# Expert order by group, and twelve picked steps instead of six, in a graph layer with a mixture of experts

## The chip, the cores and the metric

The kernel runs on one core of one Trainium2 chip. The metric is the device time of one execution in microseconds (us). The engines are named as the profile names them: PE (TensorE matmuls; its weight loads are PEld), DVE (VectorE), ACT (ScalarE), POOL (GpSimd) and SP (SyncE). ACT and SP also issue plain DMAs, each on a queue of its own, and POOL issues the indirect ones (gathers and scatters of rows).

## The reference, cut to what matters

A layer over 3,125 nodes with 256 features and 100,000 edges, sorted by destination. After a layer norm, an edge network gives every node the maximum over its incoming edges, a linear mixer runs over all nodes, and both are added to the input. Then comes a mixture of eight experts, of which every node takes its two best:

```python
xn = _layernorm(x, axis=-1)
x = x + gnn(xn, src, dst) + mix(xn)          # gnn: segment_max over the edges of relu(...)
xt = _layernorm(x, axis=-1)
probs = softmax(xt @ Wr + br); top_p, top_idx = top_k(probs, 2)
h = gelu(einsum('end,edh->enh', xe, W1) + b1)      # E = 8 experts, 256 -> 1024
y = einsum('enh,ehd->end', h, W2) + b2             # 1024 -> 256
out = x + (weights[:, :, None] * sel).sum(axis=1)  # the two chosen experts of each node
```

All data are float32. The weights of one expert (W1 and W2) are 2 MB.

## The kernel before

**Edges.** The edges lie in reverse order of their destination, so that nodes with high numbers are finished first. They are cut into four groups of columns, `STEPS = (263, 209, 157, 98)`; the nodes are handled in the groups `GROUPS = ((11, 25), (4, 11), (1, 4), (0, 1))` of tiles of 128 nodes. For each step POOL gathers 128 rows of a table `b_d` into a window `g` (line 111), and DVE folds it into a running maximum (`fold`, line 386). A window holds up to eight steps; SP stores it to `s_d` in DRAM once it is folded (`folding`, line 1457). There are five window buffers (`WN`). After the last step of a group, `last_rows` gathers from `s_d` the row at which each node ends (tile `r`), `carry` takes maxima across the 128 lanes (lines 393 to 410), and `token_tile` adds everything up, normalizes, and computes the routing.

**The last group of edges** belongs to node tile 0 alone. Its last six steps (`KEPT = 6`) are not stored. A row that ends in one of them is picked by a matmul instead: `last_ends` makes one 128x128 matrix of ones and zeros for each such step (line 1364, in `end_ones(j)`), sums them with matmuls of one column (line 1369) to learn which nodes end there, and `pick_ends` multiplies the matrix with the folded rows, accumulating in one bank (line 1381). ACT reads the sum as `kept` (line 1386), and DVE takes the maximum of it and the gathered `r` (line 459).

**Experts.** The class `Stream` runs the experts of node groups 0, 1 and 2. A lot is 256 rows of one expert in groups 0 and 1 (two lots an expert in group 0) and 128 rows in group 2. So there are 24 uses of an expert, numbered q = 0 to 23, with the experts in order 0 to 7 in each group. One unit of `Units.run` has eight steps: in each, PE makes a piece of the hidden layer (`hp`, line 644), ACT applies gelu (line 646), and PE adds a piece of the second product of the unit before (`yp`, line 668). In step 4, PE brings in the rows of the next unit (`trf`); in group 2 these are picked from chip by matmuls (line 739) with matrices that DVE makes (line 730). The bias of the second product is line 812, and ACT copies the result out (line 813).

There are three weight buffers: `w` and the two halves of `big`. Use q has buffer q mod 3. At step 7 of use q, `next_w(q + 2)` asks for the weights of use q + 2, in four parts of 512 KB (two of W1, two of W2); the ACT queue issues one part at step 7 and the others at steps 0, 2 and 5 of the next unit, right behind the gelu of that step. Every one of the 24 uses loads its 2 MB.

Node tile 0 comes last and runs all eight experts densely (`dense_tile`), in the order `DENSE = (5, 6, 7, 0, 1, 2, 3, 4)`: 5, 6 and 7 still lie in the three buffers, and five experts are loaded for it. Meanwhile `combine` gathers for the other nodes the two expert results (`g<-ys_d,from_i`), DVE adds them (line 1402), and SP writes `out`.

**Order.** PE, DVE, ACT and SP follow an order written out when the program is built: a clock of the builder ticks with each gather, tasks are due at given times, and `room()` spaces the units by an estimate of PE's time. Each engine then runs its list strictly in order. POOL has its own order of gathers (`behind`). Every plain DMA has one of eight completion counters in turn, and a DMA is issued when the last one on its counter has landed.

Of the kernel before, what the change touches and what calls it, by code (L numbers as in the profile page):

```python
# [14 lines left out]
OP = mybir.AluOpType  # L15
# [4 lines left out]
P = 128  # L20
# [4 lines left out]
D = 256  # L25
# [8 lines left out]

DENSE = (5, 6, 7, 0, 1, 2, 3, 4)
# [20 lines left out]
KEPT = 6  # L56
# [15 lines left out]
def gps_layer(ctx: ExitStack, tc: tile.TileContext, x, src, dst, thetaT, phiT, gbias, wq, wkvT,  # L72
# [608 lines left out]
    class Stream:  # L681


        def __init__(self, wts, act, ps):
            self.wts, self.act, self.ps = wts, act, ps
            self.lots, self.through, self.open = [], set(), True
            self.held = {}
            self.parts = []

        def add(self, g):  # L690
            self.lots += [(g, e, h) for e in range(E) for h in range(CAPS[g] // LOT[g])]
# [6 lines left out]
        def two(self, what, v):  # L698

            g, e, h = self.lots[2 * v]  # L700
            rows = what[g][e * CAPS[g]:e * CAPS[g] + 2 * LOT[g]]
            return rows.rearrange("(k p s) d -> p k s d", p=self.half(2 * v), k=2 * LOT[g] // CAPS[g])
# [29 lines left out]
        def turn(self, u):  # L732
            if ("hot", u) in self.held and ("tr", u) not in self.held:
                tr = self.held["tr", u] = self.ps.tile([P, 2, ROWS], F32, name="trf", bufs=1)
                i0, i1 = GROUPS[G - 2]
                hot = self.held["hot", u]
                for c in range(2):
                    for i in range(i0, i1):
                        nc.tensor.matmul(tr[:, c, 0:CAPS[G - 2]], xn2(i)[:, c * P:(c + 1) * P], hot[:, i - i0, :],
                                         start=(i == i0), stop=(i == i1 - 1))  # L740
                on_pe(1.5)
                if u + 1 == len(self.lots):
                    dense_half(0, 0, xn_lo[:, 1:1 + FC, :].rearrange("p i d -> p (i d)"), nc.scalar)
            elif ("xs", u // 2) in self.held and ("tr", u) not in self.held:
                tr = self.held["tr", u] = self.ps.tile([P, 2, ROWS], F32, name="trf", bufs=1)
                n = self.half(u)
                for c in range(2):
                    for r in range(2):
                        nc.tensor.transpose(tr[:, c, r * n:(r + 1) * n],  # L749
                                            self.held["xs", u // 2][0:n, u % 2 * 2 + r, c * P:(c + 1) * P],  # L750
                                            ident[0:n, 0:n])
                on_pe(1.2)
# [9 lines left out]

        def next_w(self, q, parts=None):
            if q < (G - 1) * E:
                self.held["w", q] = load_w(self.wts[q % 3], q % E, nc.scalar, parts)
# [5 lines left out]
        def more_w(self):  # L771
            while "firsts" not in clock:
                yield 1
            for k in range(1, 3):
                self.next_w(k)
                yield 25

        def go(self):
            units = Units(self.ps, self.act)
            u, q = 0, -1  # L780
            self.next_w(0)
            start(self.more_w())
            yield 25
            while True:
# [24 lines left out]
                def done(r, yp, u=u, ys=ys):  # L809
# [3 lines left out]
                    nc.scalar.copy(ys[0:n, u % 2 * PARTS[g] + r, :], yp[0:n, :])  # L813
# [10 lines left out]
                if h == 0:  # L824
                    q += 1
                    if q:
                        between[7] = lambda: (self.next_w(q + 2, self.parts), self.part())
# [3 lines left out]
                w1t, w2t = self.held["w", q]  # L831
# [3 lines left out]
            for k in range(3):  # L835
                dense_w[DENSE[k]] = self.held["w", q - 2 + k]
# [123 lines left out]
    def loads():  # L960
# [18 lines left out]
        move(nc.scalar, kept[:, STEPS[G - 1] - KEPT:STEPS[G - 1], :], zero.to_broadcast([P, KEPT, D]))  # L979
# [349 lines left out]
    dense_w = {}  # L1329

# [5 lines left out]
    def next_dense(k):  # L1336

        if k < 3:
            e = DENSE[k + 5]
            dense_w[e] = load_w(at_hand["w"][k], e, nc.scalar)  # L1340
# [3 lines left out]
    def end_ones(j):  # L1344
        of = xn_lo[:, SPLIT - 2:SPLIT, :] if j < 4 else xn_hi[:, 12:14, :]
        return of.rearrange("p i (c k) -> p (i c) k", k=P)[:, j % 4, :]

    def last_ends():
# [14 lines left out]
        for j in range(KEPT):  # L1363
            nc.vector.tensor_scalar(end_ones(j), row, float(1 + P * COL[g] + STEPS[g] - KEPT + j), None, op0=OP.is_equal)
            yield 1
        yield 2
        here_p = mm.tile([P, 1], F32, name="mm")
        for j in range(KEPT):
            nc.tensor.matmul(here_p, end_ones(j), ones[:, 0:1], start=(j == 0), stop=(j == KEPT - 1))
# [7 lines left out]
    def pick_ends(j, rows):  # L1377
# [3 lines left out]
        nc.tensor.matmul(ends["p"][:, 0:D], end_ones(j), rows, start=(j == 0), stop=(j == KEPT - 1))  # L1381
        on_pe(0.5)
        if j == KEPT - 1:
# [51 lines left out]
    def starts(g):  # L1435

        most = STEPS[g] - KEPT
        n = -(-most // W)
        at = [most * k // n for k in range(n + 1)] + [most + 4, STEPS[g]]
        if g == G - 1:  # L1440
            at.remove(most + 4)
        return [(a, b - a) for a, b in zip(at, at[1:])]

    def folding():

        for g in range(G):
            last = None
            rows = s_d[1 + P * COL[g]:1 + P * COL[g + 1], :].rearrange("(p t) d -> p t d", t=STEPS[g])
            for w, (t0, n) in enumerate(starts(g)):
                for j in range(n):  # L1450
# [3 lines left out]
                    if g == G - 1 and t0 + j >= STEPS[g] - KEPT:  # L1454
                        start(pick_ends(t0 + j - STEPS[g] + KEPT, last), clock["now"] + 0.5)
                if g < G - 1 or t0 + n < STEPS[g]:
# [204 lines left out]
```

## Time and profile before

| what | value |
|---|---|
| time, median of 3 runs | 1211.97 us (1210.92 to 1213.29) |
| time of the profiled execution | 1210.82 us |
| its span (first to last instruction) | 1209.0 us |
| mean granted TensorE clock | 0.86 |
| busy share of PE, PEld, DVE, ACT, POOL | 80%, 55%, 63%, 28%, 71% |
| DMA over the span | 305.46 MB, 253 GB/s |
| 512 KB parts of expert weights: issues on `big`, on `w` | 56, 28 |
| last gather of `b_d` rows starts | 1102.90 us |
| first matmul of an expert, group 0 / group 1 / group 2 | 594 / 881 / 1036 us |
| first expert matmul of the dense tile | 1136.55 us |
| last result of the dense tile on DVE | 1202.71 us |

How to read it: in the timeline a row is one run of equal instructions with its start and its length in us, and in brackets the idle time before it and what ended it. The chain of waits goes back from the last instruction to whatever released it. Windows give the busy time of each engine in a stretch, then the granted clock, the busy share of the DMA engines and the GB/s that they moved. PE counts a float32 matmul as two passes, so that a step of the hidden layer (two matmuls) shows as x4.

### The profile page before, as it was taken

To read this page: it belongs to the slowest core of one execution; us is meant where nothing else is said; L and a number is where in the kernel's file an instruction comes from. 1 tells how busy PE (TensorE), PEld (TensorE's weight loads), DVE (VectorE), ACT (ScalarE), POOL (GpSimd) and SP (SyncE) were. 2 spreads that over 40 slices of the span, in tenths; PEclk is the share of its full clock that TensorE was granted. 3 is DMA by queue.
4 is the path that set the end of the run, shared out by engine and by line. 5 is a ranking of instruction groups with operands and counts; after the bars stand their busy time and mean duration, and the time that the engine had idled before them with its cause. 6 is when DMAs were issued, how large, how long until landed. Compare 5 with 4: busy or idle time off the path is not lost.

```text
span 1209.0 us, 13723 instructions
## 1 busy us (share of the span) xinstructions
PE 967.2 (80%) x4062; PEld 670.0 (55%) x4062; DVE 758.9 (63%) x2255; ACT 333.4 (28%) x796; POOL 854.7 (71%) x879
## 2 busy tenths in 40 slices
PE   6428888787389445586599999999889999889796
PEld 5314443343144123332388888877678886778696
DVE  7698898899977999934333331786433336543443
ACT  4301232222011012311233333333133334333241
POOL 6677777777777477777777776774777767774734
PEclk9758998889579655568699999999989998889898
DMA  8756776655765755664668897774889996999593
GB/s 276 248 164 211 280 264 204 220 184 195 235 223 200 266 176 172 237 240 168 197 222 319 305 308 253 258 273 171 286 294 351 375 349 228 331 395 382 174 353 118
DMA packets 96366, 305.46 MB, mean 253 GB/s; under 512 B 19798, under 2 KB 39503, under 8 KB 85658
## 3 DMA queue, kind: packets, MB, share of 16 engines
q0 software_dynamic: 42400, 115.28, 30.4%
q1 hardware_dynamic: 25564, 107.09, 22.7%
q10 hardware_dynamic: 28318, 82.13, 19.2%
q8 instruction: 34, 0.56, 0.2%
q14 instruction: 50, 0.41, 0.1%
HBM read 183.66 MB, written 120.75 MB: 252 GB/s over the span
## 4 chain that ended last, share of the span: by engine, by line
PE 56%; DVE 20%; DMA 9%; issue 9%; POOL 2%; ACT 2%; ACTq 0%; DVEq 0%; SPq 0%; POOLq 0%
PE hp L644 17%; PE yp L668 16%; DVE g L386 5%; DVE ring L1108 4%; PE mm L423 3%; DMA g<-b_d,srcI 3%; DMA big<-in_w 3%; PE yp L812 2%; POOL g L111 2%; PE k L1140 2%; PE bp L261 2%; PE k L1080 2%; PE v L1140 2%; PE banks L1104 2%; PE mm L421 1%
## 5 line engine op out<-in xcount | busy, mean ns | idle before, releaser
L111 POOL DMA_INDIRECT g<-b_d,srcI x727 | 712.2, 980 | 227.2 <-issue 192.7
L386 DVE SCALAR_TENSOR_TENSOR g<-g,cut 128x256 f32<-128x256 f32 x723 | 349.9, 484 | 238.3 <-DMA g<-b_d,srcI 227.2
L646 ACT ACTIVATE ring<-hp,sm 128x256 f32<-128x256 f32 (+1 forms) x320 | 137.8, 432 | 297.9 <-PE hp L644 294.5
L644 PE MATMUL hp<-xe,big 128*128 128x256 f32 (+1 forms) x800 | 180.7, 351 | 10.1 <-DMA big<-in_w 5.1
L668 PE MATMUL yp<-big,ring 128*128 128x256 f32 x640 | 169.3, 382 | 0.0
L644 PEld LDWEIGHTS hp<-xe,big 128*128 128x128 f32 x800 | 140.8, 199 | 34.5 <-issue 13.6
L668 PEld LDWEIGHTS yp<-big,ring 128*128 128x128 f32 x640 | 115.3, 190 | 18.0 <-issue 5.6
L1108 DVE CUSTOM_DVE_ANT_0 ring<-big,banks 128x1024 bf16<-128x1024 f32 (+1 forms) x102 | 101.6, 996 | 24.5 <-PE banks L1104 24.3
L668 PE MATMUL yp<-w,ring 128*128 128x256 f32 x352 | 100.7, 406 | 0.0
L644 PE MATMUL hp<-xe,w 128*128 128x256 f32 (+1 forms) x416 | 96.1, 359 | 2.5 <-DMA w<-in_w 1.4
L644 PEld LDWEIGHTS hp<-xe,w 128*128 128x128 f32 x416 | 73.0, 197 | 14.9 <-issue 3.9
L668 PEld LDWEIGHTS yp<-w,ring 128*128 128x128 f32 x352 | 67.7, 203 | 11.5 <-issue 3.6
L111 POOL DMA_INDIRECT g<-ys_d,from_i x48 | 46.4, 966 | 31.0 <-DMA out<-g 16.8
L1104 PE MATMUL banks<-ring,row_of 16*128 16x512 bf16 (+1 forms) x90 | 30.7, 415 | 44.1 <-DVE big L1108 44.1
L1104 PEld LDWEIGHTS <-row_of 16*128 16x128 bf16 x112 | 7.7, 97 | 80.9 <-DVE big L1108 54.3
L111 POOL DMA_INDIRECT r<-s_d,end_i x25 | 24.5, 979 | 39.5 <-DMA s_d<-g 22.9
L760 ACT ACTIVATE xe<-trf,sm 128x256 f32<-128x256 f32 (+1 forms) x64 | 30.8, 535 | 40.6 <-PE trf L749 32.4
L749 PE MATMUL trf<-ident,xn_hi 128*128 128x128 f32 x96 | 15.4, 286 | 31.2 <-DMA xn_hi<-xs_d 31.2
L812 PE MATMUL yp<-b_sb,ident 8*128 8x256 f32 x112 | 39.3, 431 | 0.0
L1104 PE MATMUL trf<-ring,row_of 16*128 16x512 bf16 (+1 forms) x22 | 11.6, 525 | 34.2 <-DVE big L1108 34.2
L1140 PE MATMUL v<-wkv,xn_hi 128*128 128x512 f32 x56 | 33.7, 733 | 2.7 <-ACT vn L1145 2.4
L1152 ACT ACTIVATE rsk<-var,eps 128x16 f32<-128x16 f32 x25 | 7.7, 308 | 100.2 <-DVE var L1149 100.2
(316 smaller groups left out, 1363.2 us busy)
## 6 DMA issues: line engine op xcount, KB each, us to landing
s_d<-g SPq DMA_DIRECT2D x73, 1024.0 KB, 4.7
big<-in_w ACTq DMA_DIRECT2D x56, 512.0 KB, 7.6
s_d<-g SPq DMA_DIRECT2D x17, 896.0 KB, 5.0
w<-in_w ACTq DMA_DIRECT2D x28, 512.0 KB, 9.3
g<-b_d,srcI POOLq DMA_INDIRECT x727, 3.8
big<-in_w ACTq DMA_DIRECT2D x4, 2048.0 KB
xn_hi<-xs_d ACTq DMA_DIRECT2D x12, 512.0 KB, 5.2
xs_d<-zero ACTq DMA_DIRECT2D x8, 512.0 KB, 4.9
```

The costliest lines, as they stand in the source:

```text
L111: got = nc.gpsimd.indirect_dma_start(out=to, out_offset=None, in_=table, in_offset=row_index(index))
L261: nc.tensor.matmul(bp, xnT(i, c), wb[:, c, :], start=(c == 0), stop=(c == 1))
L386: nc.vector.scalar_tensor_tensor(g[:, j, :], last, cut[:, t:t + 1], g[:, j, :], op0=OP.add, op1=OP.max)
L423: nc.tensor.matmul(am, xnT(i, c), am_w[:, c, :], start=False, stop=False)
L644: nc.tensor.matmul(hp[:, 0:n], w1t[:, c, f, :], xe[:, c, 0:n], start=(c == 0), stop=(c == 1))
L646: nc.scalar.activation(hT[f][:, 0:n], hp[:, 0:n], AF.Gelu, bias=sm[:, 4 + f, e:e + 1])
L668: nc.tensor.matmul(yp[r][0:part, :], hT[q][:, r * part:(r + 1) * part], w2t[:, q, :], start=(q == 0), stop=(q == FC - 1 and self.whole))
L760: nc.scalar.activation(xe[:, c, 0:n], self.held["tr", u][:, c, 0:n], AF.Identity, bias=sm[:, 2 + c, e:e + 1], scale=sm[:, c, e:e + 1])
L812: nc.tensor.matmul(yp[0:n, :], ident[0:E, e:e + 1].to_broadcast([E, n]), b2_sb, start=False, stop=True)
L1104: nc.tensor.matmul(mask_p[:, at:to], row_of[:, k:k + 1].to_broadcast([FIRST, P]), no_edge[:, i0 * P + at:i0 * P + to], start=True, stop=True)
L1108: nc.vector.tensor_tensor_reduce(unread[:, 0:n], bT[:, h, i0 * P:i0 * P + n], mask_p[:, 0:n], 1.0, NEG, op0=OP.add, op1=OP.max, accum_out= ...
L1140: nc.tensor.matmul(to, xnT(i, c), wkv[:, c, k * INNER:(k + 1) * INNER], start=(c == 0), stop=(c == 1))
```

## The change

Two things are changed at once.

The order of the experts differs by group (`ORDERS`). Group 0 ends with experts 5, 6 and 7 on chip, and group 1 now begins with 6, 7, 5; group 1 ends with 1, 2, 3 on chip, and group 2 begins with 2, 3, 1. `plan()` works out at build time which of the three buffers holds which expert at each use and which use issues a load. Loads are still asked for two uses ahead, at step 7. The uses 8, 9, 10 and 16, 17, 18 load nothing. Group 2 ends with 5, 6, 7 as before, and the dense tile takes them from the buffers in which they now lie (`dense_slot`).

The last group of edges keeps its last twelve steps on chip instead of six (`KEPT_LAST`): the last two windows, of six steps each, are not stored, and twelve matrices are made, summed and multiplied. The matrices of the further steps lie in `xn_hi`. The rows of `s_d` that are never written are filled with zeros early on, for twelve steps instead of six.

```diff
+ORDERS = ((0, 1, 2, 3, 4, 5, 6, 7), (6, 7, 5, 4, 0, 1, 2, 3), (2, 3, 1, 0, 4, 5, 6, 7))
-KEPT = 6
+KEPT, KEPT_LAST = 6, 12
...
         def add(self, g):
-            self.lots += [(g, e, h) for e in range(E) for h in range(CAPS[g] // LOT[g])]
+            self.lots += [(g, e, h) for e in ORDERS[g] for h in range(CAPS[g] // LOT[g])]
...
+        def plan(self):
+            uses = [e for order in ORDERS for e in order]
+            self.uses, self.slot, self.loads = uses, {}, {}
+            at = [None] * 3
+            for q in range(-3, len(uses)):
+                self.loads[q] = []
+                ahead = [k for k in range(max(q, 0), len(uses)) if uses[k] not in at]
+                if ahead:
+                    wanted = set(uses[max(q, 0):ahead[0]])
+                    free = [k for k in range(3) if at[k] not in wanted]
+                    if free:
+                        at[free[0]] = uses[ahead[0]]
+                        self.loads[q].append((uses[ahead[0]], free[0]))
+                self.slot[q] = {e: k for k, e in enumerate(at) if e is not None}
         def next_w(self, q, parts=None):
-            if q < (G - 1) * E:
-                self.held["w", q] = load_w(self.wts[q % 3], q % E, nc.scalar, parts)
+            for e, k in self.loads.get(q, ()):
+                self.held["w", k] = load_w(self.wts[k], e, nc.scalar, parts)
...
-                        between[7] = lambda: (self.next_w(q + 2, self.parts), self.part())
+                        between[7] = lambda q=q: (self.next_w(q, self.parts), self.part())
...
             for k in range(3):
-                dense_w[DENSE[k]] = self.held["w", q - 2 + k]
+                dense_w[DENSE[k]] = self.held["w", self.slot[q][DENSE[k]]]
+                dense_slot.append(self.slot[q][DENSE[k]])
...
-        move(nc.scalar, kept[:, STEPS[G - 1] - KEPT:STEPS[G - 1], :], zero.to_broadcast([P, KEPT, D]))
+        move(nc.scalar, kept[:, STEPS[G - 1] - KEPT_LAST:STEPS[G - 1], :], zero.to_broadcast([P, KEPT_LAST, D]))
...
     def end_ones(j):
+        if j >= 8:
+            return xn_hi[:, 0:4, :].rearrange("p i d -> p (i d)")[:, 384 + (j - 8) * P:384 + (j - 7) * P]
...
-        for j in range(KEPT):
-            nc.vector.tensor_scalar(end_ones(j), row, float(1 + P * COL[g] + STEPS[g] - KEPT + j), None, op0=OP.is_equal)
+        for j in range(KEPT_LAST):
+            nc.vector.tensor_scalar(end_ones(j), row, float(1 + P * COL[g] + STEPS[g] - KEPT_LAST + j), None, op0=OP.is_equal)
...
-        nc.tensor.matmul(ends["p"][:, 0:D], end_ones(j), rows, start=(j == 0), stop=(j == KEPT - 1))
+        nc.tensor.matmul(ends["p"][:, 0:D], end_ones(j), rows, start=(j == 0), stop=(j == KEPT_LAST - 1))
...
     def starts(g):
-        most = STEPS[g] - KEPT
+        kept = KEPT_LAST if g == G - 1 else KEPT
+        most = STEPS[g] - kept
         n = -(-most // W)
-        at = [most * k // n for k in range(n + 1)] + [most + 4, STEPS[g]]
-        if g == G - 1:
-            at.remove(most + 4)
+        at = [most * k // n for k in range(n + 1)] + [most + (6 if g == G - 1 else 4), STEPS[g]]
...
-                if g < G - 1 or t0 + n < STEPS[g]:
+                if g < G - 1 or t0 < STEPS[g] - KEPT_LAST:
                     move(nc.sync, rows[:, t0:t0 + n, :], wins[g, w][:, 0:n, :])
```

## The prediction

> **What bounds the kernel now.** I read the table of slices first, then windows by stage, then the chain of waits from group 2 on, then PE's timeline there. In groups 0 and 1 PE is full (79.84 of the 80 us from 600 to 680, 128.01 of the 130 us from 885 to 1015) and no step waits for a weight part; the gap at 861 to 881 us is a wait for `xn_hi<-xs_d`, with no weights in flight. Loads saved before 1030 us can't shorten that. Group 2 is different. The chain (start us, length us, what):
>
> ```profile
> 1054.46 12.07 DMA big<-in_w
> 1066.66 0.78 PE hp L644 x2
> 1067.47 11.80 DMA big<-in_w
> 1079.40 0.47 PE hp L644 x2
> 1079.91 10.16 DMA w<-in_w
> 1090.20 0.47 PE hp L644 x2
> 1090.70 9.68 DMA big<-in_w
> 1100.52 0.46 PE hp L644 x2
> ...
> 1117.37 3.65 PE yp L668 x16
> 1121.02 0.62 PE yp L812 x2
> 1121.65 2.80 PE am L1381 x12
> 1124.47 0.48 ACT kept L1386
> 1125.00 1.57 PE am L465 x6
> ```
>
> Four times PE waits for a weight part and then starts a use with a lone half step. From one start of such a part's flight to the next are 13.0, 12.4, 10.8 and 10.3 us (1054.46, 1067.47, 1079.91, 1090.70, 1100.98). A use that doesn't wait takes 9.2: in PE's timeline (start, length) use 18 begins at the first row below, and the last row of its step 7 is followed by 1062.83.
>
> ```profile
> 1049.84 0.95 PE L1369 MATMUL mm<-ones,xn_lo 128*128 128x1 f32 x8
> 1050.65 0.58 PE L1369 MATMUL mm<-ones,xn_hi 128*128 128x1 f32 x4
> ...
> 1053.65 0.71 PE L644 MATMUL hp<-xe,w 128*128 128x128 f32 x4
> ...
> 1062.21 0.69 PE L812 MATMUL yp<-b_sb,ident 8*128 8x256 f32 x2
> ```
>
> So the four periods hold 46.5 - 4 x 9.2 = 9.8 us of waits (3.8, 3.2, 1.6, 1.1). The DMA engines are full there. Of the 25.83 MB moved from 1037 to 1105 us, the ACT queue, which carries the weights, has this (packets, MB, share):
>
> ```profile
> q10 hardware_dynamic: 4083, 13.44, 52.8%
> ```
>
> That is 198 GB/s for weights; a use in 9.2 us wants 2.097 MB, 228 GB/s. The other queues move 12.3 MB, 181 GB/s.
>
> After the last use the chain runs through picks, `kept`, the last carry and the routing, to the dense tile at 1136.55. The dense phase moves with its start, but for one stall (DVE and POOL rows; what stands in brackets is the idle time and what ended it):
>
> ```profile
> 1168.12 0.95 POOL L111 DMA_INDIRECT g<-ys_d,from_i  x1 [16.48 <-DMA out<-g]
> ```
> ```profile
> 1181.49 0.48 DVE L1402 SCALAR_TENSOR_TENSOR g<-g,share 128x256 f32<-128x256 f32 x1 [2.11 <-DMA g<-ys_d,from_i]
> 1181.89 0.60 DVE L863 TENSOR_SCALAR xe<-xT,sm 128x128 f32<-128x128 f32 x2
> ```
>
> PE's next dense step stands behind that L863: it comes 3.74 us late, and three steps at half clock follow (1.71 against 0.88), 2.5 us more.
>
> **The loads.** The built order of the changed kernel has 24 parts fewer on the ACT queue, so the saving is real: six loads of four parts. Those of uses 8, 9, 10 lie where nothing waits: 0. Those of 16, 17, 18 lie ahead of the waits, and seven of their parts (3.67 MB) move in 1037 to 1050. The loads that PE waits for, 19 to 22, all stay, asked for with the same lead; what goes is the backlog ahead of them. Is that enough? From about 1051, when the first is asked for, to use 23's second W1 part are 4.5 loads, 9.44 MB: at 198 GB/s 47.7 us, so 1098.7, and about 2 to land, 1101. Unwaited, use 18 starts at 1052.4 (1.25 before 1053.65, as L1369 leaves use 17) and use 23 follows after five uses of 9.2, the 2.5 of L1369 below, and 2.5 for one stretch of half clock, as at 1064.8 to 1071.6 (an estimate: three steps at 1.71 instead of 0.88): 1103.4. So the waits close with 2.4 us to spare. Single parts can still be late: of the remainder, between 0 and 9.8, I take 1.0. At 228 GB/s nothing would wait; at 175 GB/s the stretch would be 54 us, and use 23 some 4 late.
>
> Can the engines give more than 380 in all? Windows (length, busy us and rows of PE, PEld, DVE, ACT, POOL, then clock, DMA share, GB/s):
>
> ```profile
> 1055.00:1080.00 25.00, 20.80 (x123) 18.03 (x122) 12.08 (x31) 7.54 (x22) 18.39 (x20) 0.86 1.03 399
> 1105.00:1110.00 5.00, 5.00 (x36) 4.23 (x35) 2.49 (x8) 2.07 (x6) 0.00 (x0) 1.00 1.04 415
> ```
>
> With 399 the weights would have 218 (399 less 181), with 415 they would have 234. The row nearest in place is the first; I keep 198, as measured over the whole stretch, for the sum, and the others for the fast side.
>
> A rule speaks against the change here. The Trainium skill, "DMA: Bandwidth & Descriptors", section "Where 436 GB/s comes from", puts the HBM limit of a core at about 358 GB/s for transfers from HBM. By that figure weights would keep 177 GB/s, the stretch would take 53 us and use 23 would be some 3 us late instead of in time, for a sum near -3. The windows above show 399 and 415, so in this trace the measurement decides.
>
> **Added on PE.** The sum of the matrices (L1369) has 24 passes for 12 and moves from use 17 to use 18: the 12 take 1049.84 to 1051.09, so +1.25, on the path as PE runs its list in order. Where PE would wait for weights anyway it costs 0, that is the other end. It waits on the DVE's matrices, six more at about 0.22 us (L1364), placed between folds of 0.48 us that follow gathers 1.25 us apart: taken as 0, 1.3 if they were in the way. Behind it on PE stand the steps of use 18 and gelu.
>
> The picks (L1381) have 24 passes for 12; the 12 took 2.80 in the chain (with the last fold long done: it ends at 1108.96). Of the twelve picks, two now fall in use 23, four among the last `yp` and six at the end; nothing hides them, since PE is full from 1101 on: +2.7. Below that is 0, if use 23 waits for its weights. The last L812 (0.62) goes from before the picks to behind six of them and the carry's transpose (L393): the same sum.
>
> On ACT `kept` now stands behind the copy of the last result (0.37) and the issue of `ys_d` (0.38), which stood ahead of it before too, but during the picks: +0.8; between 0 (if the copy falls under the carry's matmul) and 1.1.
>
> **Moved elsewhere.** SP has one store fewer, so `r` can be gathered sooner. Before, POOL waits:
>
> ```profile
> 1117.62 0.94 POOL L111 DMA_INDIRECT r<-s_d,end_i  x1 [13.77 <-DMA s_d<-g]
> ```
>
> The `ys_d` gathers behind it come some 8 to 10 us sooner. But the carry takes `r` only at 1125, released by `kept`, and DVE's adds (L1402) stand behind the dense start in its list: 0. What covers `r`: the carry would come near 1120, a gather takes 3.8 us from issue to landing (the page's median of the edge gathers), and its issue should come near 1108 to 1110. If the store let it start only after 1116, each further microsecond would count. POOL's own list is unchanged. In the dense stall fewer gathers are in flight while `out<-g` lands: four of 131 KB, at the 345 GB/s of 1150 to 1180 1.5 us. The stall can stay (0) or go with its half clock (-6.3); I take -1.0, as the 14 us landing of that store is set by 2 MB of `g<-in_w` ahead of it on SP's queue, which stay. The zero fill writes 0.75 MB more at 54 to 108 us, where POOL's gathers set the pace: 0; at 200 GB/s it would be under 3.8 us if it stood alone.
>
> **The sum**, against the profiled execution of 1210.82 (span 1209.0 and 1.82 around it): -9.8 + 1.0 + 1.25 + 2.7 + 0.8 - 1.0 = -5.05, so 1205.8. The median of the runs is 1.15 above the profiled one: 1206.9, called 1207.0.
>
> **Rivals.** (B) The weights still pace uses 21 to 23. The gathers and stores come at POOL's rate whatever PE does, and a faster PE asks for weights sooner; each use then falls short by 10.6 - 9.2 = 1.4 us, and the first W1 parts may land 4 us late. With waits of w = 4 to 6 left the sum is -2 to 0: 1210 to 1212, no measurable change. For it: the same four loads, the same lead, 52.8% share. Against: 7.0 of the 9.8 us lie in the first two periods, right behind the removed loads.
>
> (C) Slower. All the waits stay, because a part's flight (9.7 to 12 us) comes from sharing the engines with gathers and stores, not from the backlog. The flights shrink only from 12.07 to 9.68 along the group, though the removed parts are long gone by the last. Then w = 9.8 and the added 4.75 on PE and ACT is paid in full: 1216.7. It decides from w = 5.05 on (without the -1.0), and is measurable from w = 7.5, 1214.4. Against: a part that lands late delays only a use that has no slack, and the first one now starts with more.
>
> (D) The dense stall goes too, since the `ys_d` gathers have 8 us more: -5 - 5, about 1202. Against: its cause is a store behind loads on SP's queue, both of which follow the dense start.
>
> **How the numbers follow.** Forecast 0.45, B 0.24, C 0.17, D 0.14. About 0.2%, 2.4 us, is what a measurement can tell from no change. Faster by more: the forecast and D, 0.59. The same: B, 0.24. Slower: C, 0.17. The range leaves out C and the far end of D: 1202.5 (the forecast with no wait left and most of the stall gone) to 1213.0 (B with 1 us of the unpriced edits on top). The forecast's own range is 1204 to 1209.
>
> **What would show it.** Right: 12 parts fewer in group 2; the first steps of uses 19 to 23 about 9.2 us apart (one with 2.5 more), together some 9 us less; L1369 with 24 passes in 2.5 us and 24 picks; the POOL wait of 13.77 mostly gone; the dense start near 1131.5; the late dense step still there, 3 us or so. Wrong: `big<-in_w` or `w<-in_w` pieces of 10 to 12 us in the chain again before uses 21 to 23 (B, C); PE waiting for L1364, or the carry for `r` or the last fold, which now has only 3 us to spare ahead of the last picks; a half clock in a new place; a step of groups 0 or 1 that waits for a weight part.

## The result, and the profile after

The changed kernel takes 1213.12 us, the median of 17 runs (1208.81 to 1221.05). The kernel before, run beside it on the same chip, takes 1213.26 (17 runs, 1208.18 to 1216.65). The ratio is 1.0009 with an interval of 0.999 to 1.0028: no difference that can be measured. The forecast was 1207.0 with a range of 1202.5 to 1213.0, and faster; what came is rival B's outcome, 0.1 us above the top of the range.

In some sessions the unchanged kernel too took about 1700 us; their runs are called disturbed below, and their ratios can't be carried over to 1210 us.

The profiled executions must be read with care. That of before (1210.82, span 1209.0) lies 2.4 us below the median of its 17 runs, that of after (1217.78, span 1216.0) 4.7 above its own. So the two traces differ by 7.0 us of span where the medians differ by nothing. Cut at five points that every trace has, the 7.0 us fall as follows (us from the start; "third store" is the issue of the third `out<-g` of the dense phase, "29th gather" the issue of POOL's 29th `g<-ys_d`, in the changed kernel the one behind the last long wait):

| point | before | after | stretch up to it, after less before |
|---|---|---|---|
| group 0, first `trf` | 587.14 | 588.00 | +0.86 |
| group 2, first `hp` | 1036.05 | 1035.04 | -1.87 |
| dense tile, first `hp` | 1136.55 | 1136.93 | +1.39 |
| third store issued | 1162.23 | 1163.19 | +0.58 |
| 29th gather | 1170.83 | 1178.33 | +6.54 |
| end of span | 1209.0 | 1216.0 | -0.50 |

The change acts in the third row, and there it is a loss of 1.39 us, where the forecast's terms for it add up to a gain of 4.05 (-9.8 + 1.0 + 1.25 + 2.7 + 0.8). The fifth row is the tail, which the forecast had let move with its start, but for -1.0.

**Group 2.** The chain of waits of the changed kernel (start, length, what), the answer to the one shown of before:

```profile
1065.79 10.74 DMA big<-in_w
1076.66 0.46 PE hp L645 x2
...
1097.20 9.19 DMA big<-in_w
1106.52 0.46 PE hp L645 x2
...
1120.43 2.59 PE am L1412 x12
```

Of the four weight parts that carried the chain, two are left, and they fly 10.74 and 9.19 us, against 12.07 to 9.68 before. What PE waited for weights, from the table of waits for PE between 1037 and 1110 us (us in total, times, longest), first before, then after:

```profile
PE hp L644 <- DMA big<-in_w: 5.1, 4, 1.7
PE hp L644 <- DMA w<-in_w: 1.4, 1, 1.4
```
```profile
PE hp L645 <- DMA big<-in_w: 2.6, 2, 2.2
```

So waits fell by 3.9 us, from 6.5 to 2.6. They had been put at 9.8, of which 8.8 were to go. The difference between 9.8 and 6.5 is half clock, stretches in which the granted clock is 0.50. From the first `hp` of use 18 to that of use 23, before took 1053.65 to 1109.45 = 55.80 us. Five uses of 9.19 are 45.95; the waits in them are 6.5; the remaining 3.4 are PE at half clock from 1064.8 to 1071.6, which costs half its length. After took 1051.30 to 1105.63 = 54.33: 45.95, a wait of 2.16, the sum of the matrices, which now lies in use 18, with 2.57, and again 3.4 lost to half clock, in two stretches each 3.4 us long; together 54.1. The first of these stretches begins with no wait ahead of it (PE's timeline; the row with the last passes of one column first):

```profile
1057.94 1.93 PE L1400 MATMUL mm<-ones,xn_hi 128*128 128x1 f32 x16
...
1060.35 1.06 PE L669 MATMUL yp<-big,ring 128*128 128x256 f32 x2
```

A pair of `yp` passes takes 0.60 at full clock and 1.06 here. The first of the windows that were shown of before (length, busy time and rows of PE, PEld, DVE, ACT, POOL, then clock, DMA share, GB/s) now reads:

```profile
1055.00:1080.00 25.00, 22.84 (x141) 20.30 (x140) 10.93 (x30) 7.28 (x21) 18.91 (x21) 0.88 0.97 354
```

The clock is 0.88 against 0.86. The DMA engines moved 354 GB/s against 399, and were busy for 0.97 of it against 1.03: the removed loads are gone, and yet the parts that PE waits for still need 9 to 11 us. The weights' queue from 1037 to 1105 shows that they are gone, 10.07 MB for 13.44 (packets, MB, share):

```profile
q10 hardware_dynamic: 3154, 10.07, 40.1%
```

Behind use 23 the picks take 2.83 us more than before (24 passes for 12) and `kept` stands 0.84 later behind them. With waits at -3.9, the sum at +1.3 and these two, group 2 should be 1.1 us longer; it is 1.39.

**The tail.** POOL's waits from 1105 us on (start, length, what; in brackets the wait and what ended it):

```profile
1113.19 0.94 POOL L112 DMA_INDIRECT r<-s_d,end_i  x1 [8.02 <-DMA s_d<-g]
1149.38 0.94 POOL L112 DMA_INDIRECT g<-ys_d,from_i  x1 [5.07 <-DMA out<-g]
1164.52 0.95 POOL L112 DMA_INDIRECT g<-ys_d,from_i  x1 [12.85 <-DVE g L1433]
1178.33 0.94 POOL L112 DMA_INDIRECT g<-ys_d,from_i  x1 [11.61 <-DMA out<-g]
```

`r` and the `ys_d` gathers behind it come 4.4 us sooner, where the forecast had 8 to 10, and nothing comes of it, as forecast. But where POOL waited once, 16.48 us, it now waits three times. The last wait, for a store, ends at 1178.33; before, the same gather was issued at 1170.83. DVE's adds follow the gathers, the next `xe` (L891) stands right behind one of them in DVE's list, at 1187.79, and PE behind `xe`:

```profile
1188.23 1.19 PE L645 MATMUL hp<-xe,w 128*128 128x128 f32 x4 [8.70 <-issue]
```

The late dense step is 8.70 us late for 3.74. By itself that says little of the change: the next sections show that this stretch has another length in every trace.

### The profile page after: what moved, and what is told of

It is laid out like the page before. It is cut to its first block, busy times and chain, and to the rows that moved or that the text cites. A ratio compares the mean times of both kernels' runs of the same rounds, so it can differ in the third digit from the quotient of the medians.

```text
span 1216.0 us, 13741 instructions
## 1 busy us (share of the span) xinstructions
PE 973.1 (80%) x4086; PEld 675.7 (56%) x4086; DVE 761.0 (63%) x2261; ACT 332.9 (27%) x796; POOL 850.0 (70%) x879
## 4 chain that ended last, share of the span: by engine, by line
PE 59%; DVE 17%; issue 10%; DMA 8%; POOL 4%; ACT 2%; ACTq 0%; DVEq 0%; SPq 0%; POOLq 0%
PE hp L645 18%; PE yp L669 18%; DMA g<-b_d,srcI 5%; DVE g L387 5%; POOL g L112 3%; DVE ring L1136 3%; PE mm L424 3%; PE yp L839 3%; PE bp L262 2%; DMA big<-in_w 2%; PE v L1168 2%; PE k L1168 1%; PE mm L422 1%; PE banks L1132 1%; PE k L1108 1%
## 5 line engine op out<-in xcount | busy, mean ns | idle before, releaser
L645 PE MATMUL hp<-xe,big 128*128 128x256 f32 (+1 forms) x768 | 173.8, 352 | 3.5 <-DMA big<-in_w 2.6
L645 PEld LDWEIGHTS hp<-xe,big 128*128 128x128 f32 x768 | 134.9, 198 | 25.1 <-issue 8.3
L645 PE MATMUL hp<-xe,w 128*128 128x256 f32 (+1 forms) x448 | 103.9, 362 | 10.8 <-issue 8.7
L645 PEld LDWEIGHTS hp<-xe,w 128*128 128x128 f32 x448 | 80.5, 203 | 25.8 <-issue 11.7
L757 PE MATMUL trf<-ident,xn_hi 128*128 128x128 f32 x96 | 15.4, 286 | 27.2 <-DMA xn_hi<-xs_d 27.2
L119 POOL DMA_INDIRECT xs_d<-xn_hi,slot_i x28 | 29.7, 1059 | 8.5 <-issue 7.9
```

What stands on the lines that cost most here:

```text
L119: put.append(nc.gpsimd.indirect_dma_start(out=table, out_offset=row_index(index), in_=of, in_offset=None))
L645: nc.tensor.matmul(hp[:, 0:n], w1t[:, c, f, :], xe[:, c, 0:n], start=(c == 0), stop=(c == 1))
```

## The experiments

The theories, by mechanism:

- **Backlog** (the forecast's). PE waits in group 2 because the removed loads stand ahead of those that are needed. Then the orders alone bring most of the gain, and the twelve steps alone bring the loss.
- **Flight** (rival C's mechanism). A part takes about 10 us from issue to landing because three queues share the engines, backlog or not. Then waits stay wherever a part is asked for late, and asking for W1 sooner removes them.
- **Half clock.** The 24 one-column passes of the sum bring the half clock at 1060.1. Then one matmul in their place removes it, and the twelve steps alone show it too.
- **Tail.** The dense stall, not group 2, sets the difference: through `xe` on DVE behind the adds, or through `out<-g` landing late among 2 MB loads of 16 KB packets.

**1. The orders alone** (six kept steps as before):

```diff
-KEPT, KEPT_LAST = 6, 12
+KEPT, KEPT_LAST = 6, 6
...
-        at = [most * k // n for k in range(n + 1)] + [most + (6 if g == G - 1 else 4), STEPS[g]]
+        at = [most * k // n for k in range(n + 1)] + [most + 4, STEPS[g]]
+        if g == G - 1:
+            at.remove(most + 4)
```

> The new expert orders with six picked steps, as before: 24 weight parts fewer and no added matmul. Theory 1 (the waits mostly close; what ate the gain is the added work on PE and stretches of half clock): the dense tile starts 5 to 7 us earlier than before, one wait for a weight part of about 2 us is left in group 2, ratio to before about 0.995. Rival 2 (fewer loads give nothing, since the parts of the five loads that stay are as late as ever): waits of 6 us or more are left in group 2, ratio 0.999 to 1.001.

> The new expert orders alone, once more, since in the first call every kernel, the kernel before too, took some 1700 us. With the kernel before near 1213 us: theory 1 (the waits mostly close; the added work on PE and half clock ate the gain) expects the dense tile to start 5 to 7 us earlier and a ratio of about 0.995; rival 2 (the loads that stay are as late as ever) 6 us or more of waits in group 2 and 0.999 to 1.001.

> The new expert orders with six picked steps, for one profile on another chip. If the kernel before takes near 1213 us here: theory 1 (the waits mostly close) expects the dense tile to start 5 to 7 us earlier than 1136.5 and one wait for a weight part of about 2 us in group 2; rival 2 (the parts that stay are as late as ever) 6 us or more of such waits. If it takes near 1700 us: the stages before group 2 are stretched and group 2 is read by itself, with the same two expectations for its waits on weight parts.

> The new expert orders alone, timed. By its one undisturbed trace, theory 1 as it now stands (six loads fewer take 2.3 us out of the waits of group 2 and add two more short stretches at half clock; the dense tile starts 1 us sooner after its group 0 than before): ratio 0.998 to 1.000, within what can be told from none. Rival (the prediction's term: 9.8 us of waits go but for 1): 0.993.

> The new expert orders alone, alone on its chip. Theory 1 as it now stands (six loads fewer take 2 to 3 us out of the waits of group 2, and stretches at half clock behind the waits that stay give that back): ratio 0.998 to 1.000. Rival (the prediction's term, 9.8 us of waits that go but for 1): 0.993. The end is expected 37.7 to 38.2 us after the 29th gather of combined rows, as in the four undisturbed traces.

Runs 1, 2 and 4 were disturbed (1714 to 1735 us; ratios 1.0091, 1.0079 and 1.0003), and in their traces PE waits for no weight part in group 2, so that they say nothing on the theories.

The third, one execution of each kernel, gave 1206.64 beside 1206.37 for the kernel before. The fifth is the one that decides: 1208.45 (12 runs) beside 1209.25 (17 runs), ratio 0.9984, 0.9955 to 1.0013. By the ratio the orders alone bring 1.9 us, between a gain of 5.4 and a loss of 1.6; the forecast had put some 9 on them, which is outside this interval. Waits for weights in the two undisturbed traces (the same table of waits, 1037 to 1110 us), the third run first:

```profile
PE hp L645 <- DMA big<-in_w: 3.0, 1, 3.0
PE hp L645 <- DMA w<-in_w: 1.2, 1, 1.2
```
```profile
PE hp L645 <- DMA w<-in_w: 4.3, 2, 4.0
PE hp L645 <- DMA big<-in_w: 1.1, 1, 1.1
```

4.2 and 5.4 us of waits, with six loads fewer. Uses 18 to 23 take 55.26 and 55.34 us, against 55.80 before: the rest is half clock again (10.2 us long in the third run, 6.8 in the fifth).

**2. The twelve steps alone** (all groups in the order 0 to 7, so that all 24 loads are back):

```diff
-ORDERS = ((0, 1, 2, 3, 4, 5, 6, 7), (6, 7, 5, 4, 0, 1, 2, 3), (2, 3, 1, 0, 4, 5, 6, 7))
+ORDERS = ((0, 1, 2, 3, 4, 5, 6, 7),) * 3
```

> Twelve picked steps with the old expert orders, so that all 24 uses load. Theory 1: the added work stands on the path and nothing pays for it: sum of the matrices 1.25, picks 2.7, the later ACT read about 1, ratio 1.003 to 1.005. Rival 2 (PE waits for weights there anyway, so that the matmuls fill gaps): ratio 1.000, dense start within 1 us of 1136.5.

> Twelve picked steps with the old expert orders, alone on its chip. With the kernel before near 1210 us, theory 1 expects the added work to stand on the path as in the trace of the changed kernel (sum of the matrices 1.3, picks 2.8, the later ACT read 0.8, together 4.9), less what falls into the 6.5 us of waits of group 2: dense tile 2 to 5 us later after the first row of group 0 than before (549.4), ratio 1.002 to 1.004. Rival (the matmuls fill gaps): 549 to 550, ratio 1.000. The end is expected 37.7 to 38.2 us after the 29th gather of combined rows.

The first was disturbed (0.9988, 0.9946 to 1.0031). The second took 1217.55 (12 runs) beside 1212.95 (17), ratio 1.0037, 1.0011 to 1.0064: slower by 4.5 us (1.3 to 7.8), where the forecast had added 4.75. Its trace shows less. From the first `hp` of group 2 to the dense start it takes 103.05 us against 100.50: some 4.9 of added work, less 1.0 of waits and 1.7 of half clock. And the dense start is 549.29 us behind the first `trf` of group 0 against 549.41, as the rival expectation had it, because groups 0 and 1 were 2.7 us shorter in this execution (446.24 against 448.91). The two halves, -0.16% and +0.37%, add up to +0.2%, and the interval of the whole, -0.1% to +0.28%, holds that. In the trace of the twelve steps alone the backlog is back, and the waits and flights are those of the other kernels (queue from 1037 to 1105 us; the table of waits; the chain):

```profile
q10 hardware_dynamic: 4216, 13.93, 54.5%
```
```profile
PE hp L645 <- DMA big<-in_w: 5.5, 3, 3.6
```
```profile
1063.98 12.15 DMA big<-in_w
...
1096.73 9.90 DMA big<-in_w
```

With 13.93 MB of weights the waits are 5.5 us; with 10.5 to 11.2 MB (the two runs of the orders alone) they are 4.2 and 5.4. The backlog theory falls as the main cause. This run also seems to speak against the half-clock theory, since no half clock follows its 24 one-column passes. But in every trace of this case all changes of the clock, from full to half and back, lie whole multiples of 3.413 us apart, so the clock changes only at such points. In the changed kernel the 24 passes (1057.13 to 1059.87) lie whole between two of them, 1056.74 and 1060.15, and half clock follows though PE never waited. In the twelve steps alone they (1056.98 to 1059.72) are cut by the point 1059.05, with 2.07 us ahead of it and 0.67 behind, and the clock stays full. The windows from one point to the next (columns as above), first the changed kernel, then the twelve steps alone:

```profile
1056.74:1060.15 3.41, 3.41 (x33) 3.41 (x33) 0.24 (x3) 0.00 (x0) 2.69 (x3) 1.00 1.02 423
1060.15:1063.57 3.42, 3.42 (x15) 3.06 (x14) 2.22 (x7) 1.43 (x4) 2.51 (x4) 0.50 0.94 351
```
```profile
1059.05:1062.47 3.42, 3.42 (x25) 2.99 (x25) 2.08 (x8) 1.59 (x5) 2.81 (x3) 1.00 1.03 418
1062.47:1065.88 3.41, 3.41 (x22) 2.92 (x23) 1.02 (x3) 1.57 (x5) 2.50 (x4) 1.00 1.03 374
```

Two more traces, both disturbed, have 24 passes with PE busy all around them, and they agree. In experiment 5 the passes lie whole between two points (1496.38 to 1499.11 between 1496.26 and 1499.67) and half clock follows; in the first run of this experiment they are cut, 1.14 and 1.59 us, and none does. So the theory fits all four, with the place of the passes between two points as its condition. No run moved the passes to test it.

**3. One matmul for the sum.** Two comparisons on DVE make one matrix of "ends in the last twelve steps", and one matmul counts it:

```diff
+        first = float(1 + P * COL[g] + STEPS[g] - KEPT_LAST)
+        upto = tok.tile([P, P], F32, name="end_upto", bufs=1)
+        nc.vector.tensor_scalar(upto, row, first + KEPT_LAST - 0.5, None, op0=OP.is_le)
+        nc.vector.scalar_tensor_tensor(row, row, first - 0.5, upto, op0=OP.is_ge, op1=OP.mult)
         here_p = mm.tile([P, 1], F32, name="mm")
-        for j in range(KEPT_LAST):
-            nc.tensor.matmul(here_p, end_ones(j), ones[:, 0:1], start=(j == 0), stop=(j == KEPT_LAST - 1))
+        nc.tensor.matmul(here_p, row, ones[:, 0:1], start=True, stop=True)
```

> The changed kernel with one change: whether a node ends in the last twelve steps is found by two comparisons on DVE and one matmul of one column, in place of twelve such matmuls (2 passes for 24). Theory 1a (the 24 passes of one column, 2.6 us in which PE does nearly no work, bring on the half clock that follows in use 18): use 18 takes 9.4 us instead of 13.5, and the time falls by about 4 against the changed kernel, ratio to before 0.997. Rival 1b (the half clock there comes from something else): use 18 takes about 11.3, the time falls by about 2.

> The changed kernel with one matmul in place of the twelve that sum the matrices, once more. Theory 1a (the 24 passes of one column bring on the half clock in use 18): use 18 takes 9.4 us instead of 13.5, ratio to before 0.997. Rival 1b (the half clock there comes from something else): use 18 takes about 11.3, ratio 0.998 to 1.000.

Both were disturbed; the first has no ratio, the second 1.0044 (0.9996 to 1.0093). Inconclusive by themselves.

**4. `xe` of the dense tile on ACT**, out of DVE's list:

```diff
-                    nc.vector.tensor_scalar(held["xe", e][:, c, 0:P], xT[:, c, :], sm[:, c, e:e + 1],
-                                            sm[:, 2 + c, e:e + 1], op0=OP.mult, op1=OP.add)
+                    nc.scalar.activation(held["xe", e][:, c, 0:P], xT[:, c, :], AF.Identity,
+                                         bias=sm[:, 2 + c, e:e + 1], scale=sm[:, c, e:e + 1])
```

> The changed kernel with one change: in the dense tile ACT instead of DVE scales the rows of the next expert (xe), so that they no longer stand behind the combining adds in DVE's list. Theory 3 (a good part of the time, and of its scatter, is PE waiting for xe in the seventh dense expert, 8.65 us in the profiled run of the changed kernel): that wait falls under 1 us, ratio to before about 0.995 and less scatter. Rival (the adds themselves, or the yp banks that DVE frees behind them, end the kernel anyway): the wait moves to another line of the dense tile and the time stays, ratio 1.000.

> The changed kernel with the rows of the dense experts (xe) scaled by ACT instead of DVE. Theory 3 (PE's late step in the seventh dense expert, 8.65 us in the profiled run of the changed kernel and 3.74 in that of before, is xe behind DVE's combining adds): the late step is gone, with the half clock behind it, 5 to 8 us less, ratio to before 0.994 to 0.996. Rival (the adds and the yp banks that DVE frees behind them end the kernel anyway): PE waits for another line of the dense tile by as much, ratio 1.000.

Both disturbed: 1.0028 (0.9983 to 1.0072) and 1.0036 (1.0006 to 1.0066).

**5. W1 asked for sooner.** The two W1 parts of the load are issued at steps 0 and 2 of the unit behind which they stood before, and the W2 parts of the load before it at steps 5 and 7:

```diff
-                    if q:
-                        between[7] = lambda q=q: (self.next_w(q, self.parts), self.part())
+                    self.ask(q)
+                    between[7] = lambda q=q: (self.part(self.seconds), self.seconds.extend(self.next_seconds))
+                else:
+                    between[7] = lambda: self.part(self.seconds)
...
-                for f in (0, 2, 5):
-                    between[f] = lambda f=f: (self.part(), at_step.get(f, int)())
+                for f, of in ((0, self.parts), (2, self.parts), (5, self.seconds)):
+                    between[f] = lambda f=f, of=of: (self.part(of), at_step.get(f, int)())
```

> The changed kernel with the order of the weight parts changed: in each use ACT asks for the first-product parts (W1) of the load at steps 0 and 2, as soon as the first product of the use before is done, and for the second-product parts (W2) of the load before at steps 5 and 7. The first product has its parts 7 to 8 steps sooner; bytes and number of parts are the same. Theory 1 (what is left in group 2 is W1 parts that come late when a store and the ys_d rows stand in their way, with a half clock behind each wait): the waits on weight parts, 2.6 us, go to 0 and one of two half-clock stretches (1.7) goes with them, 4 us less than the changed kernel, ratio to before 0.997. Rival 2 (the queue's rate sets the pace whatever is asked first): the waits turn up at other parts, ratio 1.000.

Disturbed: 0.9785 (0.9718 to 0.9852). The gain can't be carried over: the disturbed traces have no weight waits in group 2 that it could remove, and where it came from was not settled.

**6. All four: the whole change with edits 3, 4 and 5.**

> The changed kernel with three edits together: W1 parts asked for sooner, one matmul for the sum of the matrices, xe on ACT. If the theories hold and add up: 4 for the W1 parts, 2.3 and one half clock (1.7) for the sum, 5 to 8 for xe, together 13 to 16 us less than the changed kernel, ratio to before 0.987 to 0.990. Rival (each edit only uncovers the next wait): less than half of that, 0.995 or more.

> Once more on another chip: the changed kernel with W1 parts asked for sooner, one matmul for the sum of the matrices, and xe on ACT. With the kernel before near 1210 us, theory 1 expects no wait for a weight part in group 2 and uses 18 to 22 at 9.2 to 9.5 us each (54.3 us from use 18 to use 23 in the changed kernel, then 46 to 47), the dense tile 6 to 8 us earlier after its group's start, and the late dense step gone (5 to 8 more): ratio to before 0.988 to 0.992. Rival 2 (each edit only uncovers the next wait): 0.995 or more, with the waits at other parts or other lines of the dense tile.

The first was disturbed (0.9883, 0.983 to 0.9935). The second took 1209.47 (12 runs) beside 1212.33 (17), ratio 0.9981, 0.9961 to 1.0001. It is not clearly faster than the kernel before; the expectation had 0.988 to 0.992, its rival, that each edit only uncovers the next wait, 0.995 or more. In its trace uses 18 to 23 take 1048.17 to 1095.48 = 47.31 us instead of 54.33, and the window that had waits and half clock in both kernels is full:

```profile
1055.00:1080.00 25.00, 25.00 (x168) 22.01 (x167) 10.36 (x28) 11.26 (x32) 19.21 (x20) 1.00 1.02 384
```

The DMA engines are as busy as in the other kernels (1.02), yet up to use 23 only one wait of 0.88 is left. That fits the flight theory: asked for sooner, the W1 parts of uses 18 to 22 are there in time. It is not shown by itself, as this is one trace with edits 3 and 4 in it too, and the three traces with the new orders that ask as late as before have anything from 2.6 to 5.4 of waits. Of the 7.0 us, 2.35 come from the single matmul (use 18 is 0.22 over 9.19, where the twelve took 2.57), 1.3 from waits and 3.4 from half clock. But by the start of the dense tile, counted from the first `hp` of group 2, 2.55 us of it are left (99.34 against 101.89): in and behind use 23, PE waits 0.54 and 1.13 for the last weight parts and runs at half clock twice, from 1098.0 and from 1118.5.

Of the late dense step: with `xe` on ACT no `hp` waits for it any more, but PE now waits for DVE one step further on, at the sum of the dense results `o`, which stands in the same list among the same adds (PE's timeline; two more such waits of 3.31 and 0.45 follow):

```profile
1179.00 1.22 PE L669 MATMUL yp<-big,ring 128*128 128x256 f32 x2 [4.69 <-DVE o L926]
```

So in this trace `xe` was where the stall showed, not its cause: the stretch from the third store to the 29th gather is 14.51 us here too.

**7. Dense loads in four parts.** `next_dense` loads 2 MB as four parts of 512 KB, with packets of 4 KB instead of 16:

```diff
-            dense_w[e] = load_w(at_hand["w"][dense_slot[k]], e, nc.scalar)
+            parts = []
+            dense_w[e] = load_w(at_hand["w"][dense_slot[k]], e, nc.scalar, parts)
+            for part in parts:
+                part()
```

> The kernel of all_four (W1 parts sooner, one matmul for the sum, xe on ACT) and the three 2 MB loads of the dense tile cut into four parts of 512 KB each, issued together on ACT's queue, so that their packets are 4 KB instead of 16 KB. Theory 4 (the end of the kernel hangs on the landing of the third store of combined rows, which four traces have 8.6 to 15.1 us after its issue, because its 1 KB packets take turns with 16 KB ones): that landing falls to 6 to 8 us, the end comes 5 us sooner than in all_four, ratio to before 0.992 to 0.995. Rival (the store waits for its turn by bytes or behind SP's own loads): landing 10 us or more, ratio 0.998 as in all_four.

> The kernel of all_four with the three 2 MB loads of the dense tile cut into four parts of 512 KB each (packets of 4 KB instead of 16 KB), alone on its chip. Theory 4 (the end hangs on the landing of the third store of combined rows, 8.6 to 15.7 us in five undisturbed traces, because its 1 KB packets take turns with 16 KB ones): landing 6 to 9 us, end still 37.7 to 38.2 us after the 29th gather, ratio to before 0.992 to 0.995. Rival (the store waits behind bytes, not packets, or for a completion counter): landing 10 us or more, ratio 0.997 to 0.999 as in all_four_2.

> Once more on another chip: all_four with the three 2 MB loads of the dense tile cut into four parts of 512 KB each. With the kernel before near 1210 us, theory 4 (the end hangs on the landing of the third store of combined rows, 8.6 to 15.7 us in five undisturbed traces, because its 1 KB packets take turns with 16 KB ones) expects a landing of 6 to 9 us, the end 37.7 to 38.2 us after the 29th gather, ratio 0.992 to 0.995. Rival: landing 10 us or more, ratio 0.997 to 0.999 as in all_four_2.

> The kernel before with only the three 2 MB loads of the dense tile cut into four parts each (4 KB packets instead of 16 KB). Theory 4 (the third store of combined rows sets the end and its landing is stretched by 16 KB packets): landing 6 to 8 us, 1 to 5 us less time, ratio 0.996 to 0.999 and less scatter. Rival: no change, 1.000, or slower where the further parts make a store wait for a completion counter.

The first three stand on all four edits, the last on the kernel before. All were disturbed: 0.9905 (0.987 to 0.994), 0.9914 (0.9874 to 0.9953), 0.9858 (0.9778 to 0.9938), and 0.9996 (0.9961 to 1.0031). In their traces the stretch from the third store's issue to the 29th gather is 9.4 to 13.0 us, in the ten disturbed ones without parts 8.2 to 15.4, and all four edits without parts had 0.9883. That gives the packets no support, and the ranges are too wide to rule them out. The Trainium skill, "DMA: Bandwidth & Descriptors", section "Queues, rings and completion order", says that an engine serving several queues changes between them only at the end of a packet, which is why the packets were tried; no run here shows it. The question is left open.

## Why the prediction was wrong, step by step

**The waits (-9.8 + 1.0): mis-sized, and the mechanism wrong in the main.** Two errors lie in this term. First, 9.8 was worked out as the excess of four periods over 9.2 us, and called waits; 3.4 of it was half clock. The schedule for use 23 in the same paragraph kept one stretch of half clock (2.5), but the sum removed it. It came back in each of the four undisturbed traces of this change and its halves, for 3.4 to 10.2 us, which costs half as much. Second, the remaining 6.5 was put down to backlog. That two thirds of the excess lay right behind the removed loads was taken for cause. With all loads in place the waits were 6.5 and 5.5 us, with six loads fewer 4.2, 5.4 and 2.6: on average 1.9 us less (4.1 against 6.0), with a scatter as large. This agrees with the 1.9 us that the orders alone brought. The forecast's count of bytes, 9.44 MB at 198 GB/s against PE's clock, was of a mean; PE waits for single parts, and those that it waited for in uses 18 to 23 flew 9.0 to 12.6 us with or without the backlog. (The seven parts, 3.67 MB, that the forecast lets move from 1037 to 1050 were issued then; the weights' queue moved 2.47 MB in these 13 us.) Rival B had the outcome; rival C had this mechanism, at too high a price, since not all waits stayed.

Why a part flies long in one use and not in the next was read, not tested. In four traces (the changed kernel, both of the orders alone, the twelve steps alone) the longest wait belongs to a W1 part that is issued within half a microsecond of the `ys_d` store and within some 2.5 us of an `s_d` store. In the changed kernel:

```profile
1065.33 0.38 ACTq L105 DMA_DIRECT2D ys_d<-ys  x1
1065.79 0.45 ACTq L105 DMA_DIRECT2D big<-in_w  x1
```
```profile
1065.16 0.32 SPq L105 DMA_DIRECT2D s_d<-g  x1
```

A version that stores `ys_d` later was not run.

**Added on PE and ACT (+1.25, +2.7, +0.8): right, but for half clock.** The sum of the matrices grew by 1.3, the picks by 2.83 and `kept` by 0.84, and the twelve steps alone cost 4.5 us (1.3 to 7.8) where 4.75 was added. Not priced was the stretch of half clock behind the sum, 1.7 us in the trace of the changed kernel and none in that of the twelve steps alone. No matrix was waited for, and the carry never waited for `r` or for the last fold.

**The dense stall (-1.0): not worked out.** The forecast let the dense phase move with its start; the span of this term, 0 to -6.3, had no room for a longer stall. In six undisturbed traces the stretches behind the dense start are these (us):

| kernel | dense start to third store | third store to 29th gather | 29th gather to the end |
|---|---|---|---|
| before | 25.68 | 8.60 | 38.17 |
| after | 26.26 | 15.14 | 37.67 |
| orders alone, third run | 25.91 | 10.55 | 37.78 |
| orders alone, fifth run | 25.69 | 15.71 | 38.18 |
| twelve steps alone | 25.99 | 14.64 | 37.79 |
| all four | 25.75 | 14.51 | 37.79 |

The first and the last column hardly move, whatever was changed, and whether `xe` is on DVE or ACT. The middle one runs from 8.60 to 15.71, and the two traces of one kernel, the orders alone, differ in it by 5.2 us. The profiled execution of before had the shortest of the six, so a forecast made against it started from a short tail. That this was luck is read, not shown, as there is one such trace of before: the medians of before and after differ by 0.1 us, which hardly leaves room for a tail that is always 6.5 us longer. Rival D took the stall for something that earlier gathers could remove; `r` was gathered earlier, and the stall grew. What sets the landing of that store stays open.

**Groups 0 and 1 (0): right.** No step there waits for a weight part. But the start of group 0 lies anywhere between 582.35 and 588.22 in the six traces, on the whole later where a stretch of half clock that begins near 47 us is longer (51.2 to 58.0 us), and from there to group 2 pass 443.3 to 448.9 us. Each of these, and the tail, scatters by more than the change moves.

**The base.** 1211.97 was a median of three runs. With 17 it is 1213.26, and 1.3 of the 6.1 us by which the forecast missed are this. (The dense start near 1131.5 that the forecast named as a sign took in the -1.0 of the dense stall; by its terms for group 2 it was 1132.5. It came at 1136.93.)

## What to carry to other kernels

Before an excess over the unwaited period is called a wait, take the half clock out of it: waits are what stands in brackets, the rest is clock, and it may return in a place where nothing waits. A saved load helps PE only if the loads that PE does wait for then land sooner; compare the flights of those parts along the stretch first, and if they are as long where nothing is queued ahead, ask sooner instead of loading less. Cut the end of the profile into stretches too, and profile a kernel more than once before a stall in its tail is taken as given.

## What the runs showed of the hardware that was not expected

Half clock comes in stretches of 3.4 us and their multiples (3.4, 6.8, 10.2; near 47 us 51.2, 54.6, 58.0), and the stretches of full clock between them are multiples of 3.413 us too, in every trace. In group 2 stretches of half clock followed PE waits of 1.1 to 4.0 us; waits of 0.9 to 1.4 also passed without one. The place of a wait between two points at which the clock can change doesn't settle that: 1.10 us of waiting between two such points was followed by half clock (orders alone, fifth run, at 1066.0), 1.37 was not (before, at 1092.1). The stretch at 1060.1 of the changed kernel had no wait ahead of it, but 24 one-column passes. The Trainium skill, "TensorE: Matmul & The Clock Gate", Part 1, says that the clock halves after an idle window of about 3.4 us; here most waits ahead of half clock were shorter than that, so the figure fits the length of the stretches and not the idle time that precedes them.

The 512 KB parts that PE waited for in uses 18 to 23, on engines that are busy for 0.97 to 1.04 of the time, flew 9.0 to 12.6 us in every kernel that asked for them two uses ahead, whether the weights' queue carried 10 or 14 MB in that stretch. Other parts there, where the trace has their landing, flew 5.9 to 11.7.
